# Layer norm's root on GpSimd without the sign change of the mean, and a new order of the steps, in a two-layer macaron network

## The chip, the cores and the metric

The kernel runs on one core of a Trainium2 chip. The metric is the device time of one execution in microseconds (us). A core has five engines with a queue each: TensorE (PE in the profile, its weight loads PEld), VectorE (DVE), ScalarE (ACT), GpSimd (POOL) and SyncE (SP), which here only starts DMA transfers.

## The reference

The input x has 8 sequences of 256 tokens with 128 numbers each, in float32. Six blocks follow each other, each of them reading a layer-normalized x and adding its output to x:

```python
x = x + 0.5 * L0_ffn(layernorm(x))    # soft mixture of 16 experts
x = x + L0_attn(layernorm(x))         # linear attention, elu + 1
x = x + 0.5 * L0_ffn(layernorm(x))
x = x + 0.5 * L1_ffn(layernorm(x))    # gated, two hidden 512x512 layers, gelu
x = x + L1_attn(layernorm(x))         # attention by random features
x = x + 0.5 * L1_ffn(layernorm(x))

def _layernorm(x, axis=-1, eps=1e-05):
    m = jnp.mean(x, axis=axis, keepdims=True)
    v = jnp.var(x, axis=axis, keepdims=True)
    return (x - m) / jnp.sqrt(v + eps)
```

The mixture computes logits of all tokens against 16 x 64 slot keys (the keys are normalized too), a softmax over tokens that gathers tokens into slots, per expert two products with a gelu gate and one back, and a softmax over slots that combines the experts' outputs.

## The kernel before

**Tiles.** A sequence is two tiles of 128 tokens; x stays in SBUF all the time. The 8 sequences form two groups of four. For a group the kernel runs the mixture, linear attention, the mixture again, the gated block (two sequences at a time), the feature attention, and the gated block again. The two groups are independent, so the work of one can stand among that of the other.

**Steps and order.** Nothing is left to a scheduler. The kernel first records some 2,490 steps (`Plan.step`), each with the engines that can do it, an assumed duration on each, and the cells it reads and writes. `Plan.place` then goes through the tuple `ORDER` at the top of the file: it holds every step's number once, and a negative entry stands for the step in its second choice of engine (VectorE instead of ScalarE for an evacuation, say). `place` gives each step a start by the assumed durations, chooses buffers and PSUM banks, and `issue` emits the instructions in the order of those starts. So `ORDER` and the assumed durations fix the queue of every engine. Where `place` finds TensorE idle for over 0.7 us, `idle` puts products of the identity with itself into that time (L1503, called fillers here).

**A normalization** (`normalized`) of n tiles is three kinds of steps. `stats` on VectorE takes mean and variance (L474, L475). `root` on GpSimd makes 1/sqrt(variance + eps) from the variance (L481, L483) and the negative mean (L482). `apply`, on GpSimd or VectorE, adds the negative mean and multiplies by the root (L490). There are 52 roots. An apply on VectorE makes the next step on GpSimd wait for it (`port`).

**The start.** The slot keys are normalized in four blocks, turned by TensorE (L452) and scaled into `seT` (L593 on ScalarE, L597 on VectorE). For each sequence the normalized tokens are turned (L452), evacuated with a factor and an offset (L557 ScalarE, L559 VectorE), and multiplied with the keys (L670). The logits are evacuated (L457 ScalarE, L459 VectorE); VectorE takes the maximum over tokens (L701), ScalarE the exponentials with their sums (L709), VectorE the reciprocal (L717), GpSimd the product with it (L722), and VectorE turns 32x32 blocks (L730). Then TensorE gathers tokens into slots (L749), in four 32-row parts side by side. The maximum over slots is one long reduction for the first four sequences (L783) and pairwise maxima (L687) for the others. The experts' first products (L878) need the gathers of all four sequences of a group. Behind them stand the gate (L884, ScalarE), its product (L889, VectorE), the product back (L909), the bias (L915) and a transfer; the second softmax's subtraction and exponentials are L837 (GpSimd) and L843 (ScalarE), the combination L952.

**The blocks later** use L1021, L1025 and L1029 (linear attention), L1237, L1240, L1167 and L1265 (gated block, with the subtractions L1152 on GpSimd or VectorE, the sums L1181 and the gelus L1189), L1293, L1298, L1342, L1392 and L1427 (feature attention). Normalized tokens of these blocks are turned by VectorE in 32x32 blocks (L513) and put into place by going through memory: a spill (L516) and four reads (L522), both on SyncE's queue. The experts' weights come on that queue too, 448 KB for each expert.

Of the kernel before, what the change touches and what calls it, by code (L numbers as in the profile page):

```python
# [11 lines left out]
ALU = mybir.AluOpType  # L12
# [4 lines left out]
    10, 0, 3, 2, 1, 37, 38, 6, 7, 5, 9, 8, 19, 20, 12, 13, 11, 40, 39, 41, 22, 31, -22, 23, 24,  # L17
    42, 43, 62, 63, 130, 14, 16, 131, 25, 15, 17, 18, 4, 132, 133, 134, 26, 135, 44, -29, -28, 60,
    32, -34, 83, -35, 61, 138, 139, 84, -87, 1347, 161, 29, 30, 68, 1268, 140, 141, 54, 35, -86,
    89, 90, -37, 1297, 162, 69, 146, 70, 64, 65, 66, 67, -164, 73, 142, 143, 144, 145, 87, 88, 93,  # L20
    95, 114, 71, 91, -165, 167, 165, 1269, -1272, 74, 75, 76, 94, 97, 96, 166, 175, 151, 92, 98,
    147, 136, 72, 1348, -1350, -1351, 152, 173, 77, 99, 100, 192, 104, 174, 78, 82, 176, 81,
    -1271, 1272, 1273, 105, 169, 1298, -1300, -1301, 1301, 80, 101, 79, 102, 115, 106, 137, 170,
    1274, 153, 1303, 1302, 168, 103, 1353, 182, 1354, 107, 108, 154, 1276, 171, 1278, 172, 53, 45,
    1281, 1275, 1282, 1277, 1280, 1279, 1305, 1306, 148, 183, 177, 1284, 1285, 178, 1283, 1307,
    184, 155, 109, 1304, 111, 47, 112, 113, 149, 150, 156, 179, 185, 186, 180, 46, 110, 1286,
    1309, 1308, 157, 181, 187, 193, -190, 1310, 1312, 330, 1313, 320, 158, 159, 160, 190, 1292,
    191, 188, 331, 351, 334, 335, 1315, 1314, 1311, 324, 325, 194, 1331, 1332, 332, 321, 322,
    1333, 355, 362, 333, 257, 366, 215, 367, 352, 336, 57, 353, 368, 195, 354, 356, 357, 363, 364,
    348, 349, 369, 196, 1293, 219, 216, 217, 1334, 326, 341, 323, 370, 365, 246, 197, 198, 199,  # L30
    371, 1287, 1316, 372, 373, 220, 221, 299, 1351, 1352, 1317, 337, 261, 116, 262, 218, 117, 258,
    259, 345, 346, 342, 361, 338, 204, 260, 263, 232, 288, 200, 347, 247, 343, 344, 1357, 1358,
    248, 1355, 249, 350, 250, 251, 1376, 1288, 374, 233, 1377, -1379, 1294, 252, -1380, 118, 274,
    275, 1335, 358, 359, 303, 264, -1357, 1366, 1321, 304, 305, 300, 202, 277, 265, 289, 301, 302,
    1295, 292, 208, 319, 309, 290, 1336, 212, 1322, 209, 316, 119, 1363, 1318, 1359, 317, 291,
    206, 293, 1296, 1289, 1380, -1382, 236, 237, 240, 1319, 294, 1323, 210, 1290, 211, 213, 214,
    1360, 1382, 235, 313, 314, 55, 1320, 278, 306, 307, 310, 315, 120, 311, 1337, 222, 282, 318,
    312, 279, 241, 242, 1364, 327, -1362, 1291, 283, 284, 225, 229, 280, 281, 1324, 121, 230, 124,
    122, 328, 1325, 267, 226, 256, 238, 239, 234, 271, 231, 227, 228, 268, 269, 298, 1362, 272,
    1365, 339, 308, 207, 340, 253, 295, 270, 360, 254, 243, 273, 244, 203, 123, 285, 296, 125,  # L40
    286, 1371, 1372, 223, 201, 1373, 1374, 1375, 276, 1367, 266, 1326, 1327, 205, 255, -1329,
    1389, 1390, 1392, 1393, 375, 126, 127, 1384, -1331, 1368, 1400, 50, 128, 1338, 1385, 1386,
    -1388, 1395, 56, 1401, 1402, 1369, 1370, 287, 1396, 224, 129, 1397, 329, 245, 297, 377, 454,
    1388, 1391, 1403, 1329, 1404, 1398, 1399, 376, 378, 455, 402, 456, 457, 458, -460, -461, 464,
    1383, 461, 462, 379, 380, 1394, 1405, 1408, 1409, -1407, 1517, 403, 404, 428, 429, 1407, 463,
    1475, 1518, 1519, 465, 1343, 430, 405, 1521, 1411, 467, 466, -471, -382, 471, 1522, 1520,
    1523, -383, 383, 1479, 1480, 1476, 1477, 1478, 406, 1534, 1535, 1485, 1486, 1489, 1490, 1580,
    1410, 1412, 1581, -408, -409, 409, 1582, 1481, 431, 1491, 1487, 1496, 1497, 1500, 1501, 432,
    1583, -434, 1498, 468, 412, 1499, 1506, 384, 1502, 1507, 1488, 1492, 1493, 1510, 1511, 1413,
    410, 52, 1584, 1513, 1514, 1569, 1345, 1585, 1508, 1509, 1570, 1571, 1573, 1414, 1572, 411,  # L50
    414, 1537, 1464, 1503, -435, 435, 385, 1512, 1468, 469, 1465, 1504, 388, 1466, 1467, 1586,
    387, 1574, 1575, 1469, 1470, 413, 418, 1590, 436, 415, 1415, 1591, 472, 1433, -393, 1437,
    1341, 393, 1346, 1426, 1430, 51, 437, 389, 1587, 473, 440, 445, 416, 417, 1588, 1482, 419,
    390, 391, 1559, 1416, 394, 395, 1431, 1432, 1427, 396, 397, 1560, 1592, 474, 475, 398, 399,
    1483, 386, 1428, 1429, 1524, 1525, 439, 441, 1505, 1417, 1420, 1434, 1438, 1440, 1441, 1435,
    400, 1561, 1562, 1424, 1527, 1528, 420, 1454, 1436, 442, 1531, 1484, 401, 1439, 1529, 480,
    481, 421, 443, 48, 438, 483, 1548, 49, -445, 1593, 1526, 1532, 1533, 1563, 476, 477, 1515,
    1530, 1458, 1459, 1460, 482, 478, 479, 1549, 1550, 446, 447, 1552, 484, 588, 422, 589, -486,
    1553, -592, -591, 1494, 1551, 1564, 1589, 1545, 1546, 448, 449, 1443, 1565, 1455, 1456, 1342,
    1442, 1536, 490, 423, 1538, 1554, 450, -452, 1457, -492, 496, 497, 424, 425, 488, -490, 492,  # L60
    594, 1453, 1344, 452, 1339, 1340, 1450, 1451, 499, 1418, 426, 427, 453, 500, 1452, 1447, 592,
    559, 560, -562, -563, 509, 510, 1542, 501, 493, 593, 1576, 1577, 1578, -495, 1543, 504, 1539,
    1540, 596, 597, 495, 1566, 1567, 1544, 1444, 1445, 1541, 58, 598, 498, 599, 512, 604, 1547,
    1446, -512, 1448, 1579, 600, 1449, 563, 1568, -565, 601, 1419, 603, 502, 1422, 505, 513, 514,
    1555, 1471, 1472, 1473, 1556, 1425, 1474, 607, 1461, 1462, 506, 569, 1516, 1557, 567, 605,
    570, -603, 612, 568, 571, 1558, 575, 576, 1463, 572, 574, 503, 608, 609, 573, 486, 522, 523,
    1495, 606, 565, 583, 578, 507, 517, 613, 525, 515, 614, 516, 1421, 610, 543, 1621, 611, 526,
    533, 615, 616, 1620, 579, 580, 1622, 1623, 519, 520, 581, 1423, 518, 521, 1624, -1627, -1626,
    584, 566, 1647, 1646, 1648, 585, 582, 528, 1672, 1673, 534, 586, 535, 536, 1627, 587, 577,
    1594, 529, 1595, 524, 508, 527, 530, 531, 1674, 1596, 1597, 1598, 595, -1601, 617, 619, 487,  # L70
    620, 532, 1628, 1629, 537, 538, 542, -1600, 1601, 1602, 1604, 541, 1632, -619, 1675, 1676,
    -1679, -1678, 1649, 781, 1603, 1606, 621, 1679, 1680, 1650, 1651, 1610, 1605, 544, 545, -540,
    1631, -541, 666, 1652, 1656, 1653, 546, 1607, 1633, 1608, 1609, 1634, 782, 783, 1635, 785,
    -1637, 786, 787, 1611, 1612, 623, 670, 1613, 1637, 792, 796, 793, 805, 797, 798, 547, 1654,
    1630, 622, 708, 709, 710, 712, 713, 548, 624, 714, 1614, 1615, 1681, 711, 667, 668, 784, 655,
    656, 794, 1684, 659, 795, 1683, 799, 1616, 669, 1688, 1655, 1689, 1685, 686, 671, 672, 549,
    657, 658, 660, 625, 1658, 800, 661, -1663, 802, 803, 1657, 1686, 683, 1638, 1682, 1639, 1617,
    1618, 638, 1687, 550, 1619, 639, 553, 554, 725, 1659, 1660, 760, 761, 557, 726, 642, 643, 626,
    627, 684, 673, 1661, 1698, 644, 771, 1663, 1664, 739, 640, 764, 765, 1640, 1641, 645, 641,
    555, 1699, -1702, 772, 773, 674, 1665, 1690, 1691, 743, 740, 1692, 766, 762, -1701, 763, 1666,  # L80
    649, 741, 742, 1642, 1643, 1693, 1702, 1694, -1704, 804, 775, 628, 551, 744, 745, 1706, 1667,
    776, 777, 1644, 1645, 1732, 1695, 1696, 1668, 1669, 687, 629, 1708, 774, 1714, 1733, -1736,
    1697, 1816, 1817, 685, -1819, 646, -1735, 788, 789, 1738, 1819, 778, 779, 780, 675, 647, 1670,
    1671, 1707, 1704, 1710, 648, 665, 1709, 688, 689, 729, 650, 634, 1820, -1822, 632, 651, 1711,
    1712, 690, 1736, 1782, 1783, -1786, 1737, 1717, 691, 1713, 1824, 1716, -1826, 662, 663, 652,
    653, 1715, 1829, 636, 1722, 692, 693, 556, 1718, 790, 1740, 1832, 1833, 1826, 1827, 1830,
    1828, 1719, 1835, 1741, 718, -1785, 1745, 801, 1748, 1749, 1766, 1840, 635, 630, 697, 1786,
    1742, -1744, 1836, 704, 705, 1831, 1834, 1744, 1747, 1750, 654, 1767, 676, 1837, 757, 758,
# [217 lines left out]
def macaron_kernel(ctx: ExitStack, tc: tile.TileContext, i: dict, out: bass.AP):  # L306


    nc = tc.nc
# [1278 lines left out]
```

## Time and profile before

| what | us |
|---|---|
| median of 3 runs | 716.06 (715.72 to 717.63) |
| the profiled execution | 715.34 |
| its span | 713.6 |
| TensorE busy | 705.1 |
| VectorE busy | 492.5 |
| ScalarE busy | 398.1 |
| GpSimd busy | 331.9 |
| L483, the power, 52 times | 36.3 |
| L481 and L482, 52 times each | 10.7 and 10.1 |

Busy times are of the profiled execution, between the first and the last instruction of the program (the span). Float32 products are two passes of TensorE, so that a product of the program shows twice in the profile; flips are one pass. Passes overlap, so that the sum of their lengths is more than the time they take. The granted clock was 1.00 in the whole span.

### The profile page before, as it was taken

How to read it: one execution, taken by the hardware profiler on the slowest of the kernel's cores; microseconds unless marked ns; L12 is line 12 of the kernel's file. 1: busy time of each engine (PE TensorE's matmuls, PEld its weight loads, DVE VectorE, ACT ScalarE, POOL GpSimd, SP SyncE). 2: the span in 40 equal slices, each digit the busy share in tenths (PEclk: the TensorE clock that was granted, in tenths of full speed). 3: DMA queues.
4: the chain of work that ended last, by engine and by line, in shares of the span. 5: the costliest groups of instructions: out<-in, count | busy, mean ns of one | idle time of the engine just before them, and what ended most of it. 6: DMA issues, size and time to landing. Idle time of an engine off the chain costs nothing.

```text
span 713.6 us, 14278 instructions
## 1 busy us (share of the span) xinstructions
PE 705.1 (99%) x5218; PEld 606.1 (85%) x5218; DVE 492.5 (69%) x1075; ACT 398.1 (56%) x775; POOL 331.9 (47%) x443
## 2 busy tenths in 40 slices
PE   8999999999999999999999999999999999999998
PEld 6889899998999998998889799786787878869787
DVE  6998867668998779983625444895777777865342
ACT  4978975364892638974536563365243653443421
POOL 6750947345665357465765103535444253342210
PEclk9999999999999999999999999999999999999999
DMA  4464752567263646557354121233213142151000
GB/s 131 135 194 150 210 143 56 184 183 201 65 162 90 175 128 171 126 127 232 110 184 108 45 60 23 45 82 78 65 38 75 26 113 47 38 120 44 8 1 30
DMA packets 122453, 75.00 MB, mean 105 GB/s; under 512 B 76048, under 2 KB 110224, under 8 KB 122384
## 3 DMA queue, kind: packets, MB, share of 16 engines
q1 hardware_dynamic: 122384, 74.09, 39.1%
q8 instruction: 41, 0.67, 0.4%
q14 instruction: 28, 0.23, 0.1%
HBM read 54.06 MB, written 11.62 MB: 92 GB/s over the span
## 4 chain that ended last, share of the span: by engine, by line
PE 89%; ACT 3%; DVE 3%; DMA 2%; POOL 1%; issue 1%; SPq 1%; DVEq 0%; ACTq 0%; POOLq 0%
PE ps L1167 27%; PE ps L878 14%; PE ps L952 8%; PE ps L909 7%; PE ps L749 7%; PE ps L670 5%; PE ps L1265 4%; PE ps L1237 4%; PE ps L1240 4%; ACT comb L709 2%; DMA we<-in_We 1%; PE ps L1342 1%; PE ps L1392 1%; PE ps L452 1%; PE ps L1427 1%; PE ps L1000 1%
## 5 line engine op out<-in xcount | busy, mean ns | idle before, releaser
L878 PE MATMUL ps<-slots,we 128*128 128x256 f32 x512 | 121.1, 380 | 0.8 <-DVE k L915 0.4
L878 PEld LDWEIGHTS ps<-slots,we 128*128 128x128 f32 x512 | 93.4, 190 | 13.3 <-issue 1.0
L1167 PE MATMUL ps<-comb,slots 128*128 128x256 f32 x448 | 103.4, 381 | 0.0
L1167 PE MATMUL ps<-comb,comb 128*128 128x256 f32 x448 | 103.1, 379 | 0.0
L1167 PEld LDWEIGHTS ps<-comb,slots 128*128 128x128 f32 x448 | 83.2, 190 | 13.4 <-issue 2.8
L1167 PEld LDWEIGHTS ps<-comb,comb 128*128 128x128 f32 x448 | 83.8, 190 | 12.6 <-issue 1.7
L884 ACT ACTIVATE k<-ps,small 128x256 f32<-128x256 f32 x128 | 55.8, 475 | 61.5 <-PE ps L878 52.8
L837 POOL TENSOR_TENSOR comb<-comb,k 128x1024 f32<-128x1024 f32 x32 | 75.2, 2362 | 19.1 <-DMA k<-m 8.8
L889 DVE SCALAR_TENSOR_TENSOR k<-ps,small,k 128x256 f32<-128x256 f32 x128 | 57.2, 475 | 31.2 <-ACT k L884 30.4
L722 POOL TENSOR_TENSOR comb<-comb,sm 128x1024 f32<-128x1024 f32 x32 | 60.3, 1897 | 35.7 <-DVE sm L717 28.5
L1181 DVE TENSOR_TENSOR comb<-ps,k 128x512 f32<-128x512 f32 x48 | 32.7, 686 | 56.2 <-PE ps L1167 36.7
L909 PEld LDWEIGHTS ps<-we,k 128*128 128x128 f32 x512 | 64.1, 192 | 2.9 <-issue 0.7
L709 ACT ACTIVATE comb<-comb,sm 128x256 f32<-128x256 f32 x128 | 63.5, 506 | 3.1 <-DVE sm L701 2.5
L909 PE MATMUL ps<-we,k 128*128 128x128 f32 x512 | 64.9, 275 | 0.0
L670 PE MATMUL ps<-k,seT 128*128 128x256 f32 x256 | 61.0, 382 | 1.1 <-ACT k L557 0.9
L457 ACT COPY k<-ps 128x512 f32<-128x512 f32 (+2 forms) x45 | 23.0, 517 | 67.7 <-PE ps L1167 49.2
L952 PEld LDWEIGHTS ps<-slots,comb 128*128 128x128 f32 x512 | 58.7, 192 | 1.5 <-issue 0.7
L952 PE MATMUL ps<-slots,comb 128*128 128x129 f32 x512 | 59.4, 276 | 0.1
L749 PE MATMUL ps<-comb,k 32*128 32x256 f32 x1024 | 58.9, 378 | 0.0
L749 PEld LDWEIGHTS ps<-comb,k 32*128 32x128 f32 x1024 | 53.2, 185 | 3.6 <-ACT slots L557 0.4
L670 PEld LDWEIGHTS ps<-k,seT 128*128 128x128 f32 x256 | 46.8, 190 | 8.6 <-ACT k L557 2.2
L1189 ACT ACTIVATE comb<-comb 128x512 f32<-128x512 f32 x48 | 29.2, 627 | 38.7 <-DVE comb L1181 38.5
(148 smaller groups left out, 1246.3 us busy)
## 6 DMA issues: line engine op xcount, KB each, us to landing
we<-in_We SPq DMA_DIRECT2D x64, 448.0 KB, 4.1
k<-y SPq DMA_DIRECT2D x64, 128.0 KB, 2.9
slots<-k SPq DMA_DIRECT2D x128, 64.0 KB, 2.4
t<-comb SPq DMA_DIRECT2D x8, 512.0 KB, 2.9
k<-t SPq DMA_DIRECT2D x32, 128.0 KB, 3.2
y<-k SPq DMA_DIRECT2D x16, 128.0 KB, 2.5
k<-m SPq DMA_DIRECT2D x8, 256.0 KB, 4.0
t<-k SPq DMA_DIRECT2D x16, 128.0 KB, 1.7
```

The lines of the kernel that those rows point to most:

```text
L670: mm(pl.ap[:, j, :], seT[:, 2 * u + j].rearrange("p k s -> p (k s)"), yt.ap, start=True, stop=True,)
L709: nc.scalar.activation(ex.ap[:, 4 * h + j, :], comb.ap[:, 4 * h + j, :], AF.Exp, bias=mx.ap[:, j : j + 1], accum_out=mx.ap[:, 4 + j : 5 + j],)
L722: return nc.gpsimd.tensor_tensor(ex.ap[:, part], ex.ap[:, part], mx.ap[:, 8:12].unsqueeze(2).to_broadcast([P, 4, N]), ALU.mult,)
L749: mm(po.ap[:, k], yr.ap[rows, TT * (c % 4) + c // 4, :], ex.ap[rows, :, 32 * c : 32 * c + 32], start=(c == 0), stop=(c == N // 32 - 1), ti ...
L837: return nc.gpsimd.tensor_tensor(raw, raw, mb.ap[:, k].unsqueeze(1).to_broadcast([P, 4, N]), ALU.subtract)
L878: mm(pe.ap[:, m, :], we.ap[:, ts(2 * m + c, P)], sl.ap[:, j, k, :, 0:S], start=True, stop=True,)
L884: nc.scalar.activation(ga.ap, pe.ap[:, 0, :], AF.Gelu, bias=bg[:, e, c : c + 1])
L889: nc.vector.scalar_tensor_tensor(ht.ap[:, c, :], pe.ap[:, 1, :], bu[:, e, c : c + 1], ga.ap, ALU.add, ALU.mult,)
L909: mm(po.ap[:, r, :], ht.ap[:, c, ts(r, P)], we.ap[:, ts(4 + c, P)], start=(c == 0), stop=(c == 1),)
L952: mm(po.ap[:, t, 0 : D + 1], comb.ap[:, j, ts(t, P)], eo()[:, j, q, 0 : D + 1], start=(j == 0), stop=(j == NJ - 1),)
L1167: mm(bank.ap[:, o], w(k)[:, c, ts(o, P)], rhs().rearrange("p (c n) -> p c n", c=2)[:, c, :], start=(start and o + c == 0), stop=(stop and ...
L1181: nc.vector.tensor_tensor(C(i, k)(), bank.ap.rearrange("p o n -> p (o n)"), other(), ALU.add)
```

## The change

`root` no longer makes the negative mean; `apply` subtracts the mean instead of adding its negative. The assumed duration of a root falls from 765 + 160n to 640 + 160n ns, and the whole of `ORDER` is another permutation of the same steps. Line numbers behind `root` are two lower.

```diff
 ORDER = (
-    10, 0, 3, 2, 1, 37, 38, 6, 7, 5, 9, 8, 19, 20, 12, 13, 11, 40, 39, 41, 22, 31, -22, 23, 24,
...
         def root(_):
             v = mv.ap[:, 1 : 2 * n : 2]
             eps = EPS * EPS / (1.0 + EPS) if twice else EPS
-            m = mv.ap[:, 0 : 2 * n : 2]
             made = nc.gpsimd.tensor_scalar(v, v, 1.0, eps, ALU.mult, ALU.add)
-            nc.gpsimd.tensor_scalar(m, m, -1.0, 0.0, ALU.mult, ALU.add)
             nc.gpsimd.tensor_tensor(v, v, power[:, 0:n], ALU.pow)
             return made
...
-        step({"POOL": 765 + 160 * n}, root, [mv], [mv])
+        step({"POOL": 640 + 160 * n}, root, [mv], [mv])
...
                 return (nc.gpsimd if e == "POOL" else nc.vector).tensor_scalar(
                     dst(), src(), mv.ap[:, 2 * t : 2 * t + 1], mv.ap[:, 2 * t + 1 : 2 * t + 2],
-                    ALU.add, ALU.mult,
+                    ALU.subtract, ALU.mult,
                 )
```

In the programs as built this is the difference, counted in instructions (line numbers of before):

| engine | what | before | after |
|---|---|---|---|
| GpSimd | L482 | 52 | 0 |
| TensorE | fillers, L1503 | 33 | 35 |
| TensorE | changes between 32-row or 32-column products and whole ones | 52 | 49 |
| ScalarE, VectorE | plain evacuations L457, L459 | 114, 38 | 99, 53 |
| ScalarE, VectorE | evacuations with factor and offset L557, L559 | 45, 19 | 51, 13 |
| GpSimd, VectorE | subtractions L1152 | 37, 27 | 42, 22 |
| GpSimd, VectorE | applies L490 | 74, 30 | 77, 27 |
| ScalarE, VectorE | scaling of the features' queries and keys L1302, L1304 | 4, 4 | 6, 2 |
| ScalarE, VectorE | guarded denominators L1438, L1440 | 5, 3 | 6, 2 |
| ScalarE | table loads | 67 | 72 |

The first transfers were x of the first sequence and then the first block of keys; now the keys come first. GpSimd applies both tiles of that block, behind the first three roots. VectorE's queue up to the last turn (L730) before the first experts holds 7 applies and 4 pairwise maxima (L687) before, 6 and 3 after; the rest of it is the same set of instructions in another order. In it, the second turn of the third sequence is followed by a reciprocal, two pairwise maxima and the two turns of the fourth. TensorE's queue before the first L878 holds the same products in both, and one turn of two flips (k_90) more after.

## The prediction

> **What bounds the kernel now.** I read the page first (busy time, slices, chain), then TensorE's waits, then busy time in windows of ten us, and last the timelines of the first 55 us.
>
> ```profile
> span 713.6 us, 14278 instructions
> PE 705.1 (99%) x5218; PEld 606.1 (85%) x5218; DVE 492.5 (69%) x1075; ACT 398.1 (56%) x775; POOL 331.9 (47%) x443
> PE   8999999999999999999999999999999999999998
> DVE  6998867668998779983625444895777777865342
> PE 89%; ACT 3%; DVE 3%; DMA 2%; POOL 1%; issue 1%; SPq 1%; DVEq 0%; ACTq 0%; POOLq 0%
> ```
>
> TensorE is busy 99% of the span and carries 89% of the chain. GpSimd, whose instruction goes, carries 1%. So a saving counts only where TensorE waits. All of TensorE's waits after the start come to little (who waited for whom, TensorE only; us in total, times, longest):
>
> ```profile
> PE ps L1503 <- POOL ident masks.py:199: 1.6, 1, 1.6
> PE ps L452 <- POOL k L490: 1.1, 1, 1.1
> PE ps L1298 <- DMA k<-t: 0.5, 1, 0.5
> ```
>
> Busy hides something, though: L1503 issues fillers, products of the identity with itself, where the plan expects TensorE idle. The groups by line show 66 passes of them, the last at 45 us. At the 0.112 us at which 128-column passes follow each other they are 7.4 us. Setting each other pass against the pitch of its kind (0.216 us for 256 columns, 0.112 for 128), I find some 8.4 us more of waiting before 50 us. The start thus holds nearly 16 us in which TensorE has no real work. After 55 us the windows 55 to 200, 200 to 360, 360 to 500 and 500 to 640 leave TensorE idle 0.39, 0.50, 0.00 and 0.61 us: 1.5 in all.
>
> The windows say who owns the start (columns PE, PEld, DVE, ACT, POOL):
>
> ```profile
> 20.00:30.00 10.00, 9.74 (x90) 8.49 (x92) 10.00 (x7) 9.75 (x34) 9.17 (x17) 1.00 0.48 139
> 30.00:40.00 10.00, 9.68 (x63) 7.63 (x56) 10.00 (x9) 10.00 (x29) 5.58 (x5) 1.00 0.63 174
> 40.00:50.00 10.00, 10.00 (x159) 9.00 (x161) 10.00 (x14) 7.49 (x24) 6.25 (x4) 1.00 0.56 155
> ```
>
> VectorE has no free moment from 16.7 us until 52. Its 32x32 turns (L730) release the gathers (L749), and the experts (L878) need all four. The timelines of VectorE and TensorE at the end of the start (start, length):
>
> ```profile
> 42.55 2.39 DVE L730 STREAM_TRANSPOSE comb<-comb 128x1024 f32<-128x1024 f32 x2
> 47.28 1.23 DVE L730 STREAM_TRANSPOSE comb<-comb 128x1024 f32<-128x1024 f32 x1
> 44.31 1.16 PE L1503 MATMUL ps<-ident 128*128 128x128 f32 x8
> 45.39 7.19 PE L749 MATMUL ps<-comb,k 32*128 32x256 f32 x128
> 52.51 1.99 PE L670 MATMUL ps<-k,seT 128*128 128x256 f32 x8
> 54.34 1.89 PE L878 MATMUL ps<-slots,we 128*128 128x256 f32 x8
> ```
>
> From 54.34 us on TensorE is saturated. What the change does to that moment is most of what it can do.
>
> **The root.** One root on GpSimd:
>
> ```profile
> 8.10 0.19 POOL L481 TENSOR_SCALAR sm<-sm 128x2 f32<-128x2 f32 x1
> 8.37 0.19 POOL L482 TENSOR_SCALAR sm<-sm 128x2 f32<-128x2 f32 x1
> 8.52 0.69 POOL L483 TENSOR_TENSOR sm<-sm,power 128x2 f32<-128x2 f32 x1
> ```
>
> L482 goes, and L483 can stand where L482 stood: 0.15 us earlier. The ends are 0 (L483 was waiting for L481 anyway) and 0.19 (L482's whole length); I take 0.15, the step between the two starts. 52 roots make 7.8 us of GpSimd's 331.9. GpSimd is idle 382 us, and after the start an earlier root only lengthens a wait for TensorE, so it counts in the start alone.
>
> **The apply.** Subtract in place of add has no row in this form. Among GpSimd's two-tile operations of 128x512, the multiplies (L1118) take 1270 ns and the subtracts and adds (L1130) 1271, so I take 0.
>
> **The start, walked through in the new order.** Each step is the new program's queue with the old rows' pitches: two statistics pairs 0.78, L490 0.27 on VectorE and 0.43 on GpSimd, L701 1.10, L730 1.13, L687 0.60, L783 3.65.
> - The keys' first block now comes first. Roots: the first power ends at 5.56 (5.71 before), the second at 6.6, the third at 7.65. GpSimd then applies both key tiles until 8.6, and TensorE turns them at 8.7, where the old order turned keys at 8.07. VectorE waits 0.75 us for the third root and 0.6 for the fourth (its power ends at 10.6, read at 10.85), and after two applies and three blocks of statistics starts the first L701 at 13.75. It did so at 13.74 before. Nothing is gained there.
> - The 0.52 us in which VectorE waited for a turn of keys before L597 goes, as GpSimd has those keys at 14.6 instead of 15.84. But the third L701 needs logits that TensorE starts only at 16.2, and ScalarE has evacuated them at 18.6: it starts at 18.65 instead of 18.72.
> - From there to the end of the last L730 the old queue ran 29.7 us without a gap. The new one has one L687 fewer before that point (three, not four): 29.1. The last turn ends at 47.8 instead of 48.5.
> - The third gather needs the turn that now has one reciprocal, two L687 and two L730 behind it (0.09+1.20+2.26=3.55): 44.2. It starts at 44.3 instead of 45.39, the fourth follows, and everything to the first L878 moves with it by 1.1; the last turn alone would allow 0.7.
>
> I take 1.0. The ends: 0, if ScalarE or a landing holds the new queue as much; 1.6, if the half us before L597 is kept too. What hides a worse key block is VectorE's own queue to 13.75; without that cover it costs 0.6.
>
> The programs hold 33 filler products before and 35 after, two passes each, so 0.45 us more, in time that is idle anyway: 0. One turn of two flips (k_90) stood at 65.66 us in the saturated stretch and now stands in the idle start: 0.2 gained.
>
> **Packed and whole arrays.** Each change between 32-row or 32-column products and whole ones costs something. The 128 passes of the two last gathers took 7.12 us, so 64 take 3.56; from 27.18, where 64 start, to the flip at 30.85 are 3.67. So 0.11 a change. The old order has 52 changes and the new one 49: 0.33, between 0 and twice that.
>
> **Everything after the start.** The real products are the same, and nearly every step stands elsewhere, SyncE's transfers too. Evacuations (L457, L459): 15 go from ScalarE to VectorE, six others (L557, L559) come back; five subtractions (L1152) and three applies go from VectorE to GpSimd. ScalarE gets five more table loads, 72 instead of 67, at 1.28 us 6.4 us. Its sum, 6.4 + 6x0.57 + 1.6 for three small ones - 15x0.55, is +3; VectorE's and GpSimd's, the roots taken in, come to about 0. Idle are 315, 221 and 382 us: no engine comes near a bound. These loads are hidden by what ScalarE waits for TensorE (52.8 us at L884 alone); where a load falls between a product and its only reader with no such wait, it costs up to 1.28. A load in the trace:
>
> ```profile
> 61.94 1.28 ACT L709 ACT_TABLE_LOAD   x1
> 63.24 0.51 ACT L709 ACTIVATE comb<-comb,sm 128x256 f32<-128x256 f32 x1
> ```
>
> The Trainium skill speaks against a change that adds loads: "ScalarE: Activation LUTs", What ACT_TABLE_LOAD costs, counts a drain of 1.38 us beside the 1.283, about 2.66 a switch, which would make 13.3 us of the five. The trace has the next activation 12 ns behind the load, so the measurement decides for 1.28. By the page too, the sum stays inside ScalarE's idle time.
>
> What remains are small waits where a chain is only just covered. The old order has 1.5 us; the new can have none, or several times as many. I take no difference, with ends of -1.5 and +2.5.
>
> **The sum.** The profiled execution took 715.34 us, 1.7 of it around the span of 713.6. 715.34 - 1.0 - 0.2 - 0.33 = 713.8. The median of the runs, 716.06, lies 0.7 higher, so in its terms 714.5, 0.2% faster. A measurement of this kernel can tell about 0.3% (2.15 us) from no change.
>
> **The rivals.**
> - More comes out (faster): start 1.6, flip 0.2, changes 0.66, and the 1.5 of later waits gone: 4.0, so 712.1. For it: a new order is free to close these waits. Against: L1298 waits for a copy that has to land, and nothing in the root touches it.
> - A landing becomes the bound (slower). The place is the turned squares: L513 to L522 send 32 blocks through memory and back on SyncE's queue (L516, L522), among the 64 weight loads of 448 KB. The trace has one wait of this kind, 0.54 us before L1298 at 501.80. To pass 718.2 the forecast has to lose 3.7 us, so seven of 32 blocks at 0.54 decide; with ten it is 719.9. Against: DMA engines are 30% busy or less after 360 us.
> - The order does nothing and the shorter root nothing, since VectorE's queue and not GpSimd's owns the start: 716.06.
>
> **How the numbers follow.** The forecast gets 0.45, more coming out 0.33, a landing 0.15, nothing 0.07. Faster by over 0.3% (under 713.9) is the first rival and a little of the forecast's lower side: 0.37. Slower by over 0.3% is the landing and a little of the last: 0.16. The rest, 0.47, is within. The range reaches down to the first rival's sum with 0.3 beneath, 711.8, and up to 717.8, the forecast with 2.5 of new waits and 0.8 of an unmoved start: about 0.1 is left out at either end.
>
> **What would show it.** Right: first L878 near 53.3 us; the first L701 still near 13.7; VectorE without a gap from about 19 to 47; fillers 70 passes; the power 0.27 us behind its first instruction; TensorE idle after 55 us under 3 us. Wrong: the first L878 at 54 or later, or TensorE idle several us in one window after 55, with a DMA or a table load as releaser.

## The result, and the profile after

| | us |
|---|---|
| before, median of 6 runs | 716.31 (715.46 to 717.63) |
| after, median of 6 runs | 726.12 (722.37 to 728.37) |
| ratio after / before | 1.013, 95% interval 1.0096 to 1.0165 |
| the profiled executions, before and after | 715.34 and 722.37 |

The kernel is 1.3% slower, outside the predicted range of 711.8 to 717.8. The profiled execution of after is the quickest of its six, so the trace shows 7.0 of the 9.8 us between the medians. The page's head, the two rows of slices and the chain by engine, after:

```profile
span 720.7 us, 14242 instructions
PE 707.0 (98%) x5222; PEld 608.4 (84%) x5222; DVE 495.6 (69%) x1073; ACT 404.6 (56%) x774; POOL 358.5 (50%) x399
PE   7899999999999999999999999999999999999998
DVE  5899797666998779984644444687776768855322
PE 87%; POOL 3%; ACT 3%; DMA 2%; DVE 2%; issue 1%; SPq 1%; POOLq 0%; ACTq 0%; DVEq 0%
```

GpSimd lost 52 instructions of its root and is nevertheless busy 26.6 us longer (331.9 before), and its share of the chain grew from 1% to 3%. TensorE's waits name the step:

```profile
PE ps L452 <- POOL k L488: 5.0, 5, 2.0
PE ps L1501 <- POOL ident masks.py:199: 1.6, 1, 1.6
PE ps L876 <- DMA we<-in_We: 1.3, 1, 1.3
PE ps L950 <- DMA slots<-k: 0.7, 2, 0.5
```

L452, the turn of normalized tiles, now waits five times for L488, the apply (L490 before), where it waited once. The apply in GpSimd's groups by line and shape, first in before, then in after (count, then busy us and mean ns):

```profile
L490 POOL TENSOR_SCALAR k<-x,sm 128x128 f32<-128x128 f32 x69 | 30.9, 453 | 19.3 <-DVE k L490 8.6 <-DVE k L778 6.1 <-issue 1.3
```

```profile
L488 POOL TENSOR_SCALAR k<-x,sm 128x128 f32<-128x128 f32 x71 | 56.8, 805 | 8.8 <-DVE k L488 5.3 <-DMA slots<-k 0.6
```

The same tile with subtract in place of add takes 805 ns, not 453. That is 0.35 us more for each of GpSimd's 77 applies, 27 us in all. The windows of the start (PE, PEld, DVE, ACT, POOL, granted clock):

```profile
20.00:30.00 10.00, 7.96 (x41) 7.14 (x42) 9.88 (x7) 7.96 (x26) 9.14 (x17) 0.87 0.25 77
30.00:40.00 10.00, 10.00 (x89) 8.82 (x92) 6.76 (x7) 8.43 (x25) 6.33 (x4) 0.96 0.57 161
```

VectorE, which had no gap there before, is busy 6.76 of the ten us from 30 to 40. Its timeline tells for whom it waits, and the timelines of VectorE and TensorE at the end of the start what that costs:

```profile
34.52 2.37 DVE L728 STREAM_TRANSPOSE comb<-comb 128x1024 f32<-128x1024 f32 x2 [1.96 <-POOL comb L720]
...
50.57 2.35 DVE L728 STREAM_TRANSPOSE comb<-comb 128x1024 f32<-128x1024 f32 x2
...
59.39 0.81 PE L876 MATMUL ps<-slots,we 128*128 128x256 f32 x3
```

The turn waits for the exponentials times reciprocals (L720), which stand on GpSimd behind the applies. The first experts start at 59.39 us, 5.05 later than the 54.34 of before. That is most of the 7.0.

### The profile page after: what moved, and what is told of

It reads as the page before. It is cut to its first block, busy times and chain, and to the rows that moved or that the text cites. A ratio compares the mean times of both kernels' runs of the same rounds, so it can differ in the third digit from the quotient of the medians.

```text
span 720.7 us, 14242 instructions
## 1 busy us (share of the span) xinstructions
PE 707.0 (98%) x5222; PEld 608.4 (84%) x5222; DVE 495.6 (69%) x1073; ACT 404.6 (56%) x774; POOL 358.5 (50%) x399
## 4 chain that ended last, share of the span: by engine, by line
PE 87%; POOL 3%; ACT 3%; DMA 2%; DVE 2%; issue 1%; SPq 1%; POOLq 0%; ACTq 0%; DVEq 0%
PE ps L1165 26%; PE ps L876 14%; PE ps L950 8%; PE ps L747 7%; PE ps L907 7%; PE ps L668 5%; PE ps L1235 4%; PE ps L1238 4%; PE ps L1263 3%; POOL k L488 2%; PE ps L1340 1%; POOL sm L481 1%; PE ps L1390 1%; PE ps L452 1%; PE ps L1425 1%
## 5 line engine op out<-in xcount | busy, mean ns | idle before, releaser
L876 PE MATMUL ps<-slots,we 128*128 128x256 f32 x512 | 120.8, 380 | 1.3 <-DMA we<-in_We 1.3
L876 PEld LDWEIGHTS ps<-slots,we 128*128 128x128 f32 x512 | 94.1, 190 | 15.5 <-DVE k L887 1.9
L720 POOL TENSOR_TENSOR comb<-comb,sm 128x1024 f32<-128x1024 f32 x32 | 60.3, 1895 | 45.9 <-DVE sm L715 45.8
L457 ACT COPY k<-ps 128x512 f32<-128x512 f32 (+2 forms) x41 | 21.7, 533 | 72.7 <-PE ps L1165 53.3
L950 PEld LDWEIGHTS ps<-slots,comb 128*128 128x128 f32 x512 | 58.6, 192 | 3.1 <-issue 1.9
L488 POOL TENSOR_SCALAR k<-x,sm 128x128 f32<-128x128 f32 x71 | 56.8, 805 | 8.8 <-DVE k L488 5.3
L950 PE MATMUL ps<-slots,comb 128*128 128x129 f32 x512 | 59.6, 276 | 0.8 <-DMA slots<-k 0.7
L480 POOL TENSOR_SCALAR sm<-sm 128x2 f32<-128x2 f32 x52 | 10.4, 200 | 92.3 <-DVE sm L475 56.1
```

The source lines that it names most:

```text
L488: return (nc.gpsimd if e == "POOL" else nc.vector).tensor_scalar(dst(), src(), mv.ap[:, 2 * t : 2 * t + 1], mv.ap[:, 2 * t + 1 : 2 * t + 2 ...
L720: return nc.gpsimd.tensor_tensor(ex.ap[:, part], ex.ap[:, part], mx.ap[:, 8:12].unsqueeze(2).to_broadcast([P, 4, N]), ALU.mult,)
L876: mm(pe.ap[:, m, :], we.ap[:, ts(2 * m + c, P)], sl.ap[:, j, k, :, 0:S], start=True, stop=True,)
L950: mm(po.ap[:, t, 0 : D + 1], comb.ap[:, j, ts(t, P)], eo()[:, j, q, 0 : D + 1], start=(j == 0), stop=(j == NJ - 1),)
```

## The experiments

**Which part costs: the order, the arithmetic, and where it is used.** The changed kernel has three parts: order, two-instruction root, subtract. `order_alone` keeps the new order with the old arithmetic, and `arithmetic_alone` keeps the old order with the new arithmetic. The other two keep everything new, but go back to the old arithmetic for the 12 normalizations of the start (keys, and the tokens of the first mixture), or for the other 40.

```diff
# order_alone, against after
+            m = mv.ap[:, 0 : 2 * n : 2]
...
+            nc.gpsimd.tensor_scalar(m, m, -1.0, 0.0, ALU.mult, ALU.add)
...
-                    ALU.subtract, ALU.mult,
+                    ALU.add, ALU.mult,
# start_adds, against after (later_adds: turned = not start)
+        start = not hasattr(plan, "tag") or (twice and plan.tag[1] == 0)
+        turned = start
...
+            if turned:
+                m = mv.ap[:, 0 : 2 * n : 2]
+                nc.gpsimd.tensor_scalar(m, m, -1.0, 0.0, ALU.mult, ALU.add)
...
-                    ALU.subtract, ALU.mult,
+                    ALU.add if turned else ALU.subtract, ALU.mult,
```

> The new order with the old arithmetic: the root makes the negative mean again (three instructions), the apply adds it. Theory A (the subtract makes GpSimd's apply 0.80 us instead of 0.45, and that alone is the loss; the new order is as good as the walk said): an apply on GpSimd takes 0.45 us, the first L878 stands at about 53.5 us, 714.5 to 716 in all. Theory B (the new order is worse by itself, and GpSimd's longer applies are hidden): 722 or more, first L878 near 59.

> The old order with the new arithmetic: a root of two instructions, the apply subtracts the mean. Theory A: GpSimd's applies take 0.80 us, the first L878 comes 3 to 5 us later than 54.3, 719 to 726 in all. Theory B: 716, no change.

> The changed kernel, but the 12 normalizations of the start (keys, and the first mixture's tokens of both groups; 24 applies) have the negative mean and the add; the 40 others subtract. Theory A: the first L878 at about 53.5 instead of 59.4, and some 5 us of the 10 come back: 719 to 722; what is still lost lies after 55 us. Theory B: 725, as the changed kernel.

> The other half: the start's 12 normalizations subtract, the 40 later ones add a negative mean. Theory A: first L878 near 59.4, and only the start's loss is left: 719 to 722, with TensorE's waits after 55 us as small as before (1 to 2 us). Theory B: 725.

| kernel | median us | ratio to before (95%) | first experts, us |
|---|---|---|---|
| order_alone | 720.04 (717.45 to 721.54) | 1.0052 (1.0036 to 1.0068) | 55.31 |
| arithmetic_alone | 720.61 (720.09 to 720.81) | 1.0062 (1.0049 to 1.0075) | 56.31 |
| start_adds | 722.15 (720.16 to 726.19) | 1.0092 (1.0067 to 1.0117) | 55.30 |
| later_adds | 725.07 (723.25 to 726.56) | 1.0128 (1.0109 to 1.0147) | 59.31 |

Before had a median of 716.12 beside these. Each part alone loses: the arithmetic because of the subtract (the next kernels separate it from the root), the order although it brings no dearer instruction. So for order_alone neither theory held: it is slower than A allowed and quicker than B. arithmetic_alone has A's time, with its first experts 2.0 us later and not 3 to 5. start_adds lies just outside A's 719 to 722, and its first experts stand where order_alone has them, not at 53.5; later_adds has its first experts where A put them and the time of B. Both expectations had left out the 3.9 us that the order alone loses. The new arithmetic in the start costs 725.07 - 720.04 = 5.0 us, in the other 40 normalizations 722.15 - 720.04 = 2.1; together 7.1, where after itself lies 6.1 above order_alone. So some 70% of the new arithmetic's price falls in the 12 normalizations before TensorE is saturated.

**The two parts at the intended price.** In the next two kernels the root has its two instructions and the apply adds at 0.45 us. They leave out the sign change of the mean, so they do not compute a layer norm. They tell what the change would have been worth, had the subtract cost nothing.

```diff
# new_order_two_and_add, against after
-                    ALU.subtract, ALU.mult,
+                    ALU.add, ALU.mult,
# old_order_two_and_add, against before
-            m = mv.ap[:, 0 : 2 * n : 2]
...
-            nc.gpsimd.tensor_scalar(m, m, -1.0, 0.0, ALU.mult, ALU.add)
```

> The new order with the root of two instructions and an apply that adds; the sign change of the mean is left out, for the time alone. It is the change at the price that the prediction gave the subtract (none). Theory A (the subtract is the larger part, and the new order leans on the shorter root): VectorE no longer waits before its first turns, the first L878 stands at 53.5 to 54.5 us, 716 to 718 in all, less than the 720.0 of the new order with three instructions. Theory C (the new order loses by itself, whatever the root): 719 to 721, first L878 near 55.3.

> The old order with the root of two instructions and an apply that adds; the sign change of the mean is left out, for the time alone. Both theories: the shorter root is worth little in an order made for three instructions, since VectorE's queue bounds the start: 715.3 to 716.3, first L878 at 54.0 to 54.4.

Measured: 717.60 (715.43 to 720.31), ratio 1.0017 (1.0005 to 1.0029), in the new order; 716.23 (714.39 to 718.15), ratio 0.9995 (0.9985 to 1.0006), in the old. Before had 716.63. So even at the intended price the new order is 1.0 us slower than before, and the shorter root in the old order is worth nothing that the time can tell. (Before's medians beside the experiments differ by up to 0.5 us, and differences between kernels that ran beside different ones are no better than that.) The end of the start did move about as the prediction walked it; VectorE's last double turn and TensorE in new_order_two_and_add, and TensorE in old_order_two_and_add:

```profile
44.79 2.37 DVE L728 STREAM_TRANSPOSE comb<-comb 128x1024 f32<-128x1024 f32 x2
...
53.62 1.67 PE L876 MATMUL ps<-slots,we 128*128 128x256 f32 x7
```

```profile
53.65 4.70 PE L876 MATMUL ps<-slots,we 128*128 128x256 f32 x21
```

The old order has the same first experts, 53.65 us, which its expectation had put at 54.0 to 54.4. So the 0.7 us against before comes with the shorter root in either order. In the old order it does not reach the time: in that trace TensorE is idle 3.5 us between 55 and 640 us, 1.5 in before, 1.6 of it in one wait for VectorE (L876 for L1002).

The two pairs of kernels also show why the same subtract costs twice as much in the new order: 720.61 - 716.23 = 4.4 us in the old, 726.12 - 717.60 = 8.5 in the new. The first product with the reciprocals (L722, L720) starts at

| root and apply | old order | new order |
|---|---|---|
| two instructions, add | 18.35 | 24.44 |
| three instructions, add | 19.76 | 26.23 |
| two instructions, subtract | 21.30 | 29.95 |

The new order gives GpSimd 15 applies between 8.4 us and this product. Fifteen times 0.351 is 5.3, of the 5.5 between 24.44 and 29.95. In the old order eight stand before it: 2.8, of the 2.95 between 18.35 and 21.30. VectorE's turns wait for this product, and the first experts follow: 5.77 later in the new order (53.62 to 59.39), 2.66 in the old (53.65 to 56.31). That is most of both differences; the rest lies behind the start or in executions without a trace.

**The price of a subtract by itself.** A small kernel that computes none of the reference: four repetitions of each form, with a scalar for each partition or an immediate one, on tiles of 128, 256 and 512 columns.

```diff
+            nc.gpsimd.tensor_scalar(t, src, a, b, ALU.add, ALU.mult)        # L26
+            nc.gpsimd.tensor_scalar(t, src, a, b, ALU.subtract, ALU.mult)   # L28
+            nc.gpsimd.tensor_scalar(t, src, a, b, ALU.mult, ALU.add)        # L30
+            nc.gpsimd.tensor_scalar(t, src, a, b, ALU.mult, ALU.subtract)   # L32
+            nc.vector.tensor_scalar(t, src, a, b, ALU.add, ALU.mult)        # L38
+            nc.vector.tensor_scalar(t, src, a, b, ALU.subtract, ALU.mult)   # L40
```

> Another small kernel that only runs rows of tensor_scalar on GpSimd and VectorE and copies x to the output: add then multiply, subtract then multiply, multiply then add, multiply then subtract, with two pointers and with two immediates, on 128, 256 and 512 columns. Theory A: subtract then multiply on GpSimd takes 0.80 us at 128 columns against 0.45 for add then multiply, and VectorE takes the same for both. If the price is one for each element, it is 1.4 us more at 512; if it is one for each instruction, 0.35 at every size.

Groups by line and shape, GpSimd's first (busy us, mean ns), then VectorE's:

```profile
L28 POOL TENSOR_SCALAR t<-x,sc 128x512 f32<-128x512 f32 x4 | 8.6, 2148 | 0.4
L26 POOL TENSOR_SCALAR t<-x,sc 128x512 f32<-128x512 f32 x4 | 3.3, 831 | 0.3
...
L32 POOL TENSOR_SCALAR t<-x,sc 128x128 f32<-128x128 f32 x4 | 3.2, 794 | 0.0
L28 POOL TENSOR_SCALAR t<-x,sc 128x128 f32<-128x128 f32 x4 | 3.2, 793 | 0.0
L26 POOL TENSOR_SCALAR t<-x,sc 128x128 f32<-128x128 f32 x4 | 1.8, 448 | 5.0 <-DMA x<-in_x 5.0
```

```profile
L38 DVE TENSOR_SCALAR t<-x,sc 128x128 f32<-128x128 f32 x4 | 1.4, 348 | 38.1 <-POOL t L36 38.1
L40 DVE TENSOR_SCALAR t<-x,sc 128x128 f32<-128x128 f32 x4 | 1.3, 331 | 0.0
```

The subtract's extra grows with the columns: 0.345, 0.664 and 1.317 us at 128, 256 and 512. It is a price for each element, 3.5 ns a column ((2148 - 793) / 384) against 1.0 ((831 - 448) / 384) with add. It hardly matters whether the subtract is the first operation (L28) or the second (L32), and VectorE has no such price. The Trainium skill, "GPSIMD Engine Reference", 3.1 Elementwise, counts 1.03 cycles for each element where an operation is bound by its reads and writes, at 1.2 GHz 0.86 ns as an estimate; the add comes near it, the subtract takes four times as long, and the measurement decides.

**What the new order loses behind the start.** The profiles of the new order show TensorE waiting for weights and placements (transfers that bring an expert's output into place, L922 in before's lines) between 200 and 360 us, so in the next kernels the experts' weights have seven buffers, not six.

```diff
-        "we": (6 * P + D, 6),
+        "we": (6 * P + D, 7),
```

> The new order with the old arithmetic (three instructions, add), and seven buffers for experts' weights, not six, so that a load is issued one expert earlier. Theory L (the new order's loss after 55 us is weights that land late): the wait of L878 for we at 291 us (1.6 us) goes, 718 to 719 instead of 720.0. Theory M (the chain of products is late there anyway): the wait turns into one for L889 or L915, 720.

> The new order with the root of two instructions, an apply that adds (the sign change of the mean is left out, for the time alone) and seven weight buffers. Theory L (what the new order loses after 55 us at the intended prices is mostly weights that land late): 715.5 to 716.5, level with the kernel before or just under it, first L878 at 53.6. Theory M (it is the sum of many landings, of which the weights are only one): 717 to 718.

> The kernel before with seven weight buffers, nothing else. Theory L (late weights belong to the new order): 715.8 to 716.8, no change, since the old order waits 0.2 us for weights. Theory M (a seventh buffer helps any order): 714.5 or less.

| kernel with seven buffers | median us | ratio to before (95%) | its twin with six |
|---|---|---|---|
| new_order_seven_weights (order_alone) | 718.14 (717.09 to 721.92) | 1.0031 (1.0017 to 1.0045) | 720.04 |
| new_order_add_seven (new_order_two_and_add) | 716.67 (713.96 to 717.78) | 1.0000 (0.9988 to 1.0012) | 717.60 |
| old_order_seven_weights (before) | 715.04 (714.29 to 717.98) | 0.9984 (0.9974 to 0.9995) | 716.41 |

Before had 716.63 beside the first and 716.41 beside the others. The wait in order_alone, as the chain has it, and SyncE's queue before it:

```profile
285.76 5.62 DMA we<-in_We
...
291.51 3.69 PE ps L878 x16
```

```profile
284.42 1.24 SPq L922 DMA_DIRECT2D slots<-k  x2
285.76 0.54 SPq L864 DMA_DIRECT2D we<-in_We  x1
```

The load of an expert's weights goes out at 285.76, behind two placements. It lands at 291.4, and L878 has waited 1.47 us. With a seventh buffer, with which the plan can place the load earlier, this wait is gone: L878 waits 0.2 us or less for weights in either new-order kernel. The medians fall by 1.9 and 0.9 us, the second no more than the runs scatter, and new_order_add_seven lies between what its two theories gave. Waits for placements stay (L950 for slots, 1.4 us in new_order_add_seven). That the old order too gains 0.16%, where before's trace has TensorE wait 0.2 us for weights, was not expected by either theory. The two profiled executions are 1.05 us apart, and their traces show most of that: between 55 and 640 us TensorE is idle 1.50 us in before and 0.64 here, and the waits of L1298 for a landing (0.5) and of L878 for weights (0.2) are gone. That the seventh buffer removes the first of them is not shown, nor where the rest of the 1.4 us between the medians comes from. old_order_seven_weights computes the whole reference and is the quickest one here that does, ahead of both before and after.

## Why the prediction was wrong

**The apply, taken at 0: the step that failed.** It is the term "Subtract in place of add has no row in this form", sized by L1118 and L1130. These are operations of two tiles, 1.27 us for 512 columns whether they multiply, add or subtract. The apply is an operation of one tile and two scalars, and in that form subtract costs 793 ns and add 448, at its 128 columns. The rows were the nearest in the trace and still of another form. The step said so and then set no bounds. Two rows would have given them: L490's own 453 ns below, and above the 1271 of a whole two-tile operation. That upper end is, as an estimate, 0.8 us more for each of the 15 applies ahead of the first product, 12 us, and the range would have had to reach far to the slow side. At its true price the step is worth 8.5 us in the new order (717.60 to 726.12) and 4.4 in the old.

**What hid it.** The prediction covered a worse key block by "VectorE's own queue to 13.75". GpSimd's queue was taken as following. With the subtract it leads: GpSimd has one gap between 8.4 and 29.95 us, of 0.73, and VectorE waits 1.74 us for keys, 1.40 for exponentials and 1.96 for L720. So the premise that VectorE's queue and not GpSimd's owns the start held in before and in new_order_two_and_add from some 17 us on, and not in after. Ahead of that it did not hold even in before: VectorE waits 0.97 us there for roots before its first L701 (13.74 us), and in old_order_two_and_add, with the shorter root alone, these waits are gone and that maximum starts at 13.21.

**The start's walk: near its number, in part by luck.** It gave 53.3 us for the first experts; with add and the two-instruction root they start at 53.62. The gain against before was to be 1.0 and was 0.7. The walk had nothing gained before the first L701 (13.75 said), and all of it from the order behind that. But 0.5 is gained there (13.26 measured, 14.05 in after). The order does move the queue's end: the last turn ends at 47.16 (44.79 + 2.37; 47.8 said), the third gather starts at 44.33 (44.3 said). Only the two last gathers then take 7.46 us to the next product, not 7.12, for a reason that is not shown, and the old order with the same root is as early at the first experts (53.65). With three instructions the new order is 1.0 us later there than the old (55.31 and 54.34). So it gained nothing by itself at the point that counts. Another detail of the walk was off: GpSimd's two key applies end at 9.26 us, not 8.6, as they wait 1.00 us for VectorE's apply.

**The root: right in size, and not seen in the time of the old order.** After shows the power 0.27 us behind its first instruction:

```profile
10.12 0.19 POOL L480 TENSOR_SCALAR sm<-sm 128x2 f32<-128x2 f32 x1
10.39 0.71 POOL L481 TENSOR_TENSOR sm<-sm,power 128x2 f32<-128x2 f32 x1
```

In the old order the third instruction costs 0.7 us at the first experts and nothing that the time can tell (716.23 without it, 716.63 with). In the new order, which packs GpSimd tighter, it costs 2.4 us (720.04 with it, 717.60 without): the first product with the reciprocals then starts at 26.23, not 24.44, and VectorE waits 0.61 us for it. So the new order needs the shorter root to be as quick as it is, and the price paid for that root is the subtract.

**Later waits, taken at 0 with ends of -1.5 and +2.5: a second miss.** The prediction's test was TensorE idle several us in one window after 55, with a DMA as releaser. The window from 200 to 360 us, first of new_order_two_and_add, then of after:

```profile
200.00:360.00 160.00, 156.14 (x1333) 140.29 (x1331) 124.10 (x288) 100.75 (x223) 88.63 (x90) 1.00 0.50 142
```

```profile
200.00:360.00 160.00, 157.79 (x1341) 142.42 (x1341) 127.83 (x290) 105.01 (x237) 94.68 (x93) 1.00 0.51 147
```

TensorE is idle 3.86 and 2.21 us there, 0.50 before. In the first kernel 1.9 of these end with weights and 0.7 with a placement, and 1.2 with ScalarE and GpSimd. That is the landing rival's mechanism, at weights and placements and not at the turned squares that it named; the squares' wait (L1425 for k) is 0.7 us. Between 55 and 640 us TensorE is idle 5.4 us in that trace, 3.5 in after's, 1.5 in before's, so that the first is 3.9 up and beyond the upper end. By the medians these waits take back the 0.7 that the start gained, and 1.0 us more, which is inside it. By itself this miss would have left the time within 0.3% of before.

**The rest.** 70 passes of fillers, as said. ScalarE, with five more loads, is busy 6.5 us longer, where the prediction added up 3, and TensorE's longest wait for ScalarE is 0.3 us (L1235). The flip and the changes between packed and whole products, 0.5 us together, were not measured by themselves. The rivals in which more comes out and in which nothing changes are both out.

**What stays open.** The trace of after shows 5.05 us in the start and 2.0 behind it. The other five executions take up to 6.0 us more and have no trace. The clock (last section) can be a part of it, but it does not put these executions in order: the two quickest, 722.37 and 722.87, have mean clocks of 0.997 and 1.000, the slowest, 728.37, has 0.998. What makes the difference is not shown. Nor is it shown why the new order meets more late landings behind the start.

## What to carry to other kernels

A price holds for a form: operation, engine, one tile or two, scalar or tile. Where an edit swaps only the operation, measure that form by itself before a whole queue is rebuilt on it, or bound it on both sides by the queue it stands in. To see what a dearer step costs, count how many of it stand ahead of the first result that another engine waits for: 15 times 0.35 us explained the new order, 8 times 0.35 the old. An order made for assumed durations can use up the slack of the engine that the assumption made cheap: the same subtract cost 8.5 us in the new order and 4.4 in the old. And a number that comes out near is not yet a mechanism: only the old order with the same root showed that the new order had no part in the start's gain.

## What the runs showed of the hardware

**Subtract on GpSimd.** With scalars it costs 2.5 ns more for each column than add, with immediates too (644 against 298 ns at 128 columns). Between two tiles it costs no more than a multiply, and on VectorE no more than an add.

**A lower clock behind a wait of about 2 us.** In after TensorE waits 1.97 us for GpSimd, up to 26.52. The windows behind it (the granted clock is the third number from the end), and the same for start_adds, where L881 waits 2.20 us for weights up to 292.77:

```profile
24.00:28.00 4.00, 2.03 (x12) 1.61 (x12) 4.00 (x4) 2.46 (x9) 3.68 (x7) 0.92 0.20 67
28.00:32.00 4.00, 4.00 (x18) 3.54 (x17) 2.60 (x3) 3.12 (x11) 3.90 (x5) 0.66 0.73 216
```

```profile
292.00:296.00 4.00, 3.23 (x9) 2.61 (x10) 0.98 (x2) 0.84 (x2) 0.79 (x2) 0.64 0.47 92
```

The clock falls to 0.66 and 0.64 for one window of four us. It need not: later_adds has the same wait of 1.97 us at the same place, and its clock stays at 1.00. Behind the waits of 1.5 us in order_alone (before 291.51) and 1.6 us in old_order_two_and_add (before 173.77) it stays at 1.00 too. The Trainium skill, "TensorE: Matmul & The Clock Gate", Why this matters for your kernels, asks for no gaps above some 3 us; here gaps of 2 us were followed by a fall in two of three profiles. What a fall costs depends on what bounds the place. In after's start it costs next to nothing: the first experts start at 59.39 us with it and at 59.31 in later_adds without it. In start_adds TensorE is the bound, and the 16 passes behind the wait take 5.38 us, where order_alone has 3.69 (shown above):

```profile
292.77 5.38 PE L881 MATMUL ps<-slots,we 128*128 128x256 f32 x16 [2.20 <-DMA we<-in_We]
```

Five of after's six executions have a mean clock of 0.998 or less, one of the four of later_adds with the same wait in its start, and one of the 62 of before that ran beside the experiments. A mean of 0.9975 over 720 us is 1.8 us of full clock. That is the most that such falls can explain in an average execution of after; how much of it they do is not shown.
